# Cross-attention on one core: softmax sums inverted once for each n through DMA, and two sums of A moved to the end of batch 0's step

## The chip, the cores and the metric

The kernel runs on one core of one Trainium2 chip. The metric is the device time of an execution in microseconds (us); smaller is better. A profiled execution also has a span, from the first to the last instruction that the profiler saw on the core.

## The reference

There are eight batches. `x1` and `x2` (the context) are 512 x 1024 in float32, rows c, columns n or m. What is computed for each batch is

```
q = x1^T Wq^T + bq              # 1024 x 64
k = Wk x2 + bk                  # 64 x 1024
v = Wv x2 + bv                  # 512 x 1024
attn = softmax(q k, axis=m)     # 1024 x 1024, each row n sums to 1 over m
out = v attn^T + x1             # 512 x 1024
```

Since each row of `attn` sums to 1, the bias `bv` may be added to the output once. The kernel computes `Wv (x2 attn^T)` rather than `(Wv x2) attn^T`, with unnormalized exponentials, and multiplies by the reciprocals of the softmax sums in between. It is those reciprocals that the change is about: there is one for each n, 1024 for each batch.

## The kernel before, in words

**Two products of 2 x 2 blocks.** The product y = x2 E (E the exponentials, 1024 x 1024, indexed m by n) and the product o = Wv y are each done with seven block products instead of eight, in the Strassen-Winograd way. Block products are numbered as in the table `MULT` (L259), and done by `multiply` (L269): `first(i)` in a period is product i of y, with 4 matmuls for each of two 128 x 512 accumulators; `second(i)` is product i of o, with 2 for each. The accumulators are four PSUM banks, a0, a1, c0 and c1. Bank a is opened by products 1 of each stage and taken over by 6, 5 and 3; bank c is opened by 2, by 7, and 4 goes on in it. The sums of blocks that the products need are made on VectorE: `sum_a` (L124) makes S1, S2, S3, S4 of A (the transposed x2) for each batch, each 128 x 1024; `sum_e` (L245) makes T1 to T4 of the exponentials, `sum_y` (L251) T1 to T4 of y, and `left_sums(w, ...)` those of the weights once.

**The softmax.** n is split in halves h = 0 and 1 of 512, and m lies in partitions, eight tiles of 128. `scores` (L164) makes the scores, and ScalarE copies them to SBUF. `fold` (L194) and `fold_halves` (L203) take the maximum over tiles on VectorE, and `highest` (L207) takes it over partitions with an all-reduce on GpSimd (L210), which leaves the same 512 numbers in every partition. `exponentials` (L227) subtracts it on VectorE and takes exp on ScalarE. The sums go the same way: `sums` (L334) folds on VectorE and calls `total` (L212), which adds the halves and has GpSimd add over partitions (L215) into the tile `den`, 128 x 512, of which all partitions are alike. `shares` (L217) inverts `den` in place on VectorE with one 128 x 512 RECIPROCAL (L219); the result is called `rden`.

**Where the reciprocals are used.** `evict_y` (L294) takes a finished block of y out of PSUM in up to two steps: step 1 adds the accumulator and a temporary (L308), or for block 12 multiplies the accumulator by `rden` at once (L306); step 2 multiplies by `rden` (L310). Blocks 11 and 21 use half 0, blocks 12 and 22 half 1. `evict_o` (L319) takes blocks of o out, adding `bv` and x1 (L324) and a temporary (L331), and stores them through SP's DMA queue (L332).

**The order of the work.** The order is written out by hand, and every engine runs its own instructions in that order. `head` (L349) does batch 0's scores and half of its softmax. `period` (L431) is then called for each batch s, with n the next batch, nn and nnn those after it. In it the products of s are interleaved with the softmax of n: the scores and maxima of half 0 of n stand between first(6) and first(5) (L480 to L483), its exponentials after first(5) (L489), the scores of half 1 and the sums of half 0 of n after first(3) (L497, L498), the maxima of half 1 before first(4) (L507, L508), its exponentials among the products of o. So `total(n, 0)` of a batch is made in the period of the batch before (for batch 0 at L447), and `total(s, 1)` in its own (L463). Both halves are inverted in the period of s, after first(2): `shares(s, 0)` at L458 for batch 0 and at L461 for the others, `shares(s, 1)` at L465. In the period of batch 0 VectorE has more to do than in the others, since the rest of batch 0's softmax (`head_second`, L408) and the sums of the weights (L505) lie there. There too all four sums of A of the next batch (index 1, `sum_a` at L529) stand after second(7), and before the evictions of blocks 12 and 21 of o (L532, L534); in the later periods S1 to S3 stand after the exponentials of half 0 (L491) and S4 after the T sums of y (L503).

**Queues.** SP issues the loads of x, of A and of the old x1 (`fetch_o`) and the stores. ScalarE issues the copies of q between partitions (L156). GpSimd's own DMA queue is used twice, at the start, for the biases (L366, L367).

Of the kernel before, what the change touches and what calls it, by code (L numbers as in the profile page):

```python
# [9 lines left out]
F32 = mybir.dt.float32  # L10
# [5 lines left out]
def kernel(  # L16
# [40 lines left out]
    nc = tc.nc  # L57
    P = 128
# [3 lines left out]
    H = 512  # L62
# [3 lines left out]

    const = ctx.enter_context(tc.tile_pool(name="const", bufs=1))
    sb = ctx.enter_context(tc.tile_pool(name="sb", bufs=1))
    ps_s = ctx.enter_context(
        tc.tile_pool(name="ps_s", bufs=2, space=bass.MemoryType.PSUM)  # L70
    )
# [19 lines left out]
    def left_sums(a, *ks):  # L91

        for k in ks:
            x, y, op = {
                "S1": ("21", "22", ALU.add),
                "S2": ("S1", "11", ALU.subtract),
                "S3": ("11", "21", ALU.subtract),
                "S4": ("12", "S2", ALU.subtract),
            }[k]
            nc.vector.tensor_tensor(a["21" if k == "S3" else k], a[x], a[y], op)  # L100
            if k == "S3":
                a["S3"] = a["21"]

    class Batch:
        def __init__(self, b):
            self.b = b
            self.a, self.e, self.t, self.y, self.o = {}, {}, {}, {}, {}
            self.mx, self.top, self.den, self.rden = {}, {}, {}, {}
            self.tmp, self.bank = {}, {}

    def load_x(s, x):
# [12 lines left out]
    def sum_a(s, *ks):  # L124
        for k in ks:
            if k != "S3":
                s.a[k] = sb.tile([P, MH, C // 2], F32, tag=f"a{k}", name=f"a{k}_{s.b}")
        left_sums(s.a, *ks)
# [29 lines left out]
    def keys(s, bank=None):  # L158

        ps = project(s, "k", wk_sb, bank)  # L160
        s.k = sb.tile([P, H], F32, tag="k", name=f"k_{s.b}", bufs=2)
        nc.scalar.activation(s.k, ps, AF.Identity, bias=bk_sb)
# [31 lines left out]
    def fold(s, h, i, kind, op, ps=None):  # L194

        e = s.e[h]
        if i == 1:
            s.mx[h] = sb.tile([P, 2, H], F32, tag="fold", name=f"{kind}_{s.b}_{h}", bufs=2)
        f = s.mx[h]
        new = e[:, :, i, :] if ps is None else ps  # L200
        nc.vector.tensor_tensor(f, e[:, :, 0, :] if i == 1 else f, new, op)  # L201

    def fold_halves(s, h, op):  # L203
        f = s.mx[h]
        nc.vector.tensor_tensor(f[:, 0, :], f[:, 0, :], f[:, 1, :], op)  # L205

    def highest(s, h):  # L207
        fold_halves(s, h, ALU.max)
        s.top[h] = sb.tile([P, H], F32, tag="top", name=f"top_{s.b}_{h}", bufs=2)
        nc.gpsimd.partition_all_reduce(s.top[h], s.mx[h][:, 0, :], P, ReduceOp.max)  # L210

    def total(s, h):  # L212
        fold_halves(s, h, ALU.add)
        s.den[h] = sb.tile([P, H], F32, tag="den", name=f"den_{s.b}_{h}", bufs=3)
        nc.gpsimd.partition_all_reduce(s.den[h], s.mx[h][:, 0, :], P, ReduceOp.add)  # L215

    def shares(s, h):  # L217
        s.rden[h] = s.den[h]
        nc.vector.reciprocal(s.rden[h], s.den[h])  # L219

    def first_exponentials(s, g, i):

# [10 lines left out]
    def right_sums(t, k):  # L233

        x, y = {"T1": ("12", "11"), "T2": ("22", "T1"), "T3": ("22", "12"), "T4": ("21", "T2")}[k]
        nc.vector.tensor_tensor(t[k], t[x], t[y], ALU.subtract)  # L236

    def open_t(s):
        for n in ("T1", "T2", "T4"):
            s.t[n] = sb.tile([P, MH, H], F32, tag=f"e{n}", name=f"e{n}_{s.b}")  # L240
        e0, e1 = s.e[0], s.e[1]
        s.t |= {"11": e0[:, 0], "12": e1[:, 0], "21": e0[:, 1], "22": e1[:, 1]}
        s.t["T3"] = s.t["12"]

    def sum_e(s, *ks):  # L245
        for i in (0, 2):
            part = {n: v[:, i : i + 2, :] for n, v in s.t.items()}
            for k in ks:
                right_sums(part, k)
# [44 lines left out]
    def evict_y(s, k, steps=(1, 2)):  # L294

        bank, add = RESULT[k]
        rden = s.rden.get(int(k[1]) - 1)
        if 1 in steps:
            s.y[k] = sb.tile([P, 2, H], F32, tag=f"y{k}", name=f"y{k}_{s.b}")
        y = s.y[k]  # L300
        for step in steps:
            for j in range(2):
                ps = s.bank[bank, j]
                if add is None:
                    if step == 1:
                        nc.vector.tensor_tensor(y[:, j, :], ps, rden, ALU.mult)  # L306
                elif step == 1:
                    nc.vector.tensor_tensor(y[:, j, :], ps, s.tmp[add, j], ALU.add)  # L308
                else:
                    nc.vector.tensor_tensor(y[:, j, :], y[:, j, :], rden, ALU.mult)  # L310
# [8 lines left out]
    def evict_o(s, k):  # L319
        bank, add = RESULT[k]  # L320
        for j in range(2):
            c = 2 * (int(k[0]) - 1) + j
            o = s.o[k, j]
            nc.vector.scalar_tensor_tensor(  # L324
                o, s.bank[bank, j], bv_sb[:, c : c + 1], o, ALU.add, ALU.add
            )
        for j in range(2):
            c, h = 2 * (int(k[0]) - 1) + j, int(k[1]) - 1
            o = s.o[k, j]
            if add is not None:  # L330
                nc.vector.tensor_tensor(o, o, s.tmp[add, j], ALU.add)  # L331
            nc.sync.dma_start(out[s.b, ts(c, P), ts(h, H)], o)  # L332

    def sums(s, h):  # L334
        for i in range(1, MH):
            fold(s, h, i, "sum", ALU.add)
        total(s, h)
# [93 lines left out]
    def period(s, n, nn, nnn):  # L431

        def first(i):
            multiply(s, "y", i, s.a, s.t, MH)

        def second(i):
            multiply(s, "o", i, w, s.y, 2)

        open_t(s)
        first(1)
        if s.b == 0:
            head_second(s, n)
        sum_e(s, "T1", "T2")
        if s.b == 0:
            total(s, 0)  # L447
        else:
            sum_e(s, "T4")
        if n:  # L450
            load_a(n, "11")
        first(2)
        if s.b == 0:
            keys(n)
            load_x(nn, x1)
            evict_y(s, "11", (1,))
            sum_e(s, "T4")
            shares(s, 0)  # L458
            evict_y(s, "11", (2,))
        else:  # L460
            shares(s, 0)  # L461
            evict_y(s, "11")
        sums(s, 1)  # L463
        sum_e(s, "T3")
        shares(s, 1)  # L465
        if n:
            load_a(n, "12", "21", "22")
        first(6)

        def next_queries():  # L470
            queries(nn)
            load_x(nn, x2)

        def next_keys():
            keys(nn)
            if nnn:
                load_x(nnn, x1)

        if n:
            scores_and(n, 0, "c", next_queries if nn else nothing)  # L480
            for i in range(1, MH):
                fold(n, 0, i, "max", ALU.max)
            highest(n, 0)  # L483
        first(5)
        fetch_o(s, "11")
        fetch_o(s, "22")
        if n:
            for i in range(MH):
                exponentials(n, 0, i)  # L489
            if s.b:  # L490
                sum_a(n, "S1", "S2", "S3")  # L491
        first(7)
        evict_y(s, "22")
        first(3)
        evict_y(s, "12")
        if n:
            scores_and(n, 1, "a", next_keys if nn else nothing)  # L497
            sums(n, 0)  # L498
        sum_y(s, "T1")
        sum_y(s, "T2")  # L500
        if n:
            if s.b:
                sum_a(n, "S4")  # L503
            else:
                left_sums(w, "S1", "S2", "S3", "S4")  # L505
            for i in range(1, MH):
                fold(n, 1, i, "max", ALU.max)  # L507
            highest(n, 1)  # L508
        first(4)
        evict_y(s, "21")  # L510
        second(1)
        sum_y(s, "T3")
        sum_y(s, "T4")
        second(6)
        fetch_o(s, "12")
        if n:
            exponentials(n, 1, 0)
            exponentials(n, 1, 1)
        second(2)
        evict_o(s, "11")  # L520
        fetch_o(s, "21")
        second(5)
        if n:
            exponentials(n, 1, 2)
            exponentials(n, 1, 3)
        second(7)
        evict_o(s, "22")
        if s.b == 0:
            sum_a(n, "S1", "S2", "S3", "S4")  # L529
        if n:  # L530
            second(3)
            evict_o(s, "12")  # L532
            second(4)
            evict_o(s, "21")  # L534
        else:
            second(4)
            evict_o(s, "21")
            second(3)
            evict_o(s, "12")
# [37 lines left out]
```

## Time and profile before

| | us |
|---|---|
| median of 3 runs | 717.13 (717.1 to 717.17) |
| the profiled execution, its own time | 716.93 |
| its span | 714.9 |
| time around the span | 2.03 |
| TensorE (PE) busy in the span | 705.6 |
| VectorE (DVE) busy | 590.2 |
| ScalarE (ACT) busy | 201.3 |
| GpSimd (POOL) busy | 97.2 |

The granted TensorE clock is 1.0 throughout. Busy time is from the first to the last moment of an instruction, and matmuls overlap, so a busy TensorE need not be one at its full rate: the distance from one group's start to the next group's start tells more. "Idle before" in a row of the timeline is how long the engine stood still ahead of it, and what it was released by. The timelines of the profile are merged rows of equal instructions: start, length, engine, line, what is written from what, count.

A period of the middle batches takes 86.93 us (first(1) of one starts at 210.75, of the next at 297.68). The period of batch 0 has in addition the projections of two more batches, and lies between 26.12 and 123.72.

### The profile page before, as it was taken

What the parts mean: (1) busy time and instruction counts of PE and PEld (TensorE: products, weight loads), DVE (VectorE), ACT (ScalarE), POOL (GpSimd) and SP (SyncE); (2) the same over time, 40 slices, a digit from 0 to 9 for tenths busy, and PEclk for the clock granted to TensorE, in tenths of its full rate; (3) what the DMA queues carried; (4) which work ended last, traced back from release to release, by engine and by line L of the source; (5) the groups of instructions that cost most, each with busy time, mean ns of one, the idle gap of its engine ahead of it and who ended that gap; (6) DMA issues with size and microseconds to landing.
All of it is one profiled execution on the core that took longest, in us unless ns stands there. A gap on an engine that the chain in (4) does not pass through costs nothing.

```text
span 714.9 us, 5407 instructions
## 1 busy us (share of the span) xinstructions
PE 705.6 (99%) x1892; PEld 299.8 (42%) x1892; DVE 590.2 (83%) x569; ACT 201.3 (28%) x271; POOL 97.2 (14%) x38
## 2 busy tenths in 40 slices
PE   8999999999999999999999999999999999999997
PEld 4333444434444434444344444443434444444443
DVE  0999899988979888798887987889887898989454
ACT  2733412043211522224231232403324034220010
POOL 0132030030200211021200202002020020301000
PEclk9999999999999999999999999999999999999999
DMA  8577132441333503435133252232601350042004
GB/s 333 210 235 256 68 147 101 156 154 46 147 146 119 189 8 141 148 118 191 58 119 127 109 191 98 108 118 89 220 0 61 117 177 0 0 161 75 0 1 147
DMA packets 34699, 87.39 MB, mean 122 GB/s; under 512 B 3952, under 2 KB 3952, under 8 KB 34672
## 3 DMA queue, kind: packets, MB, share of 16 engines
q1 hardware_dynamic: 33344, 84.95, 33.6%
q10 hardware_dynamic: 1264, 2.10, 0.9%
q8 instruction: 15, 0.25, 0.1%
q14 instruction: 12, 0.10, 0.0%
q0 software_dynamic: 64, 0.00, 0.0%
HBM read 68.42 MB, written 16.78 MB: 119 GB/s over the span
## 4 chain that ended last, share of the span: by engine, by line
PE 87%; DVE 8%; DMA 1%; issue 1%; ACT 1%; SPq 0%; POOL 0%; DVEq 0%; ACTq 0%; POOLq 0%
PE ps_ya L279 27%; PE ps_yc L279 21%; PE ps_oa L279 15%; PE ps_oc L279 11%; PE ps_s L180 5%; PE ps_k L138 3%; PE ps_q L138 3%; DVE max L201 1%; DMA x_head<-in_x_dram 1%; DVE eT L236 1%; DVE e L230 1%; DVE aS L100 1%; PE ps_sa L180 1%; DVE den L219 1%; PE ps_sc L180 1%
## 5 line engine op out<-in xcount | busy, mean ns | idle before, releaser
L215 POOL PARTITION_ALL_REDUCE den<-sum x16 | 65.3, 4081 | 433.2 <-DVE sum L205 433.2
L279 PE MATMUL ps_ya<-eT,aS 128*128 128x512 f32 x256 | 113.1, 595 | 0.0
L279 PE MATMUL ps_yc<-e,a 128*128 128x512 f32 x256 | 112.6, 592 | 0.0
L289 ACT COPY uy<-ps_ya 128x512 f32<-128x512 f32 x48 | 28.1, 588 | 233.2 <-PE ps_ya L279 233.2
L230 DVE TENSOR_TENSOR e<-e,top 128x1024 f32<-128x1024 f32 x60 | 70.0, 1219 | 13.9 <-POOL top L210 13.9
L279 PEld LDWEIGHTS ps_ya<-eT,aS 128*128 128x128 f32 x256 | 48.0, 190 | 63.8 <-issue 63.6
L279 PEld LDWEIGHTS ps_yc<-e,a 128*128 128x128 f32 x256 | 48.6, 190 | 61.6 <-issue 60.1
L324 DVE SCALAR_TENSOR_TENSOR o<-ps_oc,bv_sb,o 128x512 f32<-128x512 f32 x48 | 35.7, 749 | 41.6 <-PE ps_oc L279 41.5
L231 ACT ACTIVATE e<-e 128x1024 f32<-128x1024 f32 x60 | 62.2, 1056 | 22.2 <-DVE e L230 20.4
L289 ACT COPY uo<-ps_oa 128x512 f32<-128x512 f32 x48 | 28.1, 586 | 132.4 <-PE ps_oa L279 131.1
L189 ACT COPY e<-ps_s 128x1024 f32<-128x1024 f32 x47 | 46.7, 1027 | 61.5 <-PE ps_s L180 61.5
L279 PE MATMUL ps_ya<-e,a 128*128 128x512 f32 x128 | 56.4, 594 | 1.3 <-ACT e L225 0.8
L279 PE MATMUL ps_oc<-y,w 128*128 128x512 f32 x128 | 57.5, 592 | 0.0
L279 PE MATMUL ps_oa<-yT,w_S 128*128 128x512 f32 x128 | 57.5, 592 | 0.0
L279 PE MATMUL ps_yc<-eT,a 128*128 128x512 f32 x128 | 57.0, 598 | 0.0
L279 PE MATMUL ps_ya<-e,aS 128*128 128x512 f32 x128 | 56.2, 592 | 0.0
L219 DVE RECIPROCAL den<-den 128x512 f32<-128x512 f32 x16 | 53.6, 3349 | 0.0
L180 PE MATMUL ps_s<-q,k 64*128 64x512 f32 x188 | 47.9, 608 | 1.6 <-ACT q L347 0.8
L210 POOL PARTITION_ALL_REDUCE top<-max x16 | 30.3, 1897 | 131.3 <-DVE max L205 131.3
L308 DVE TENSOR_TENSOR y<-ps_yc,uy 128x512 f32<-128x512 f32 x48 | 31.2, 676 | 15.0 <-PE ps_yc L279 14.9
L201 DVE TENSOR_TENSOR max<-max,e 128x1024 f32<-128x1024 f32 x32 | 39.2, 1225 | 3.7 <-ACT e L187 0.5
L201 DVE TENSOR_TENSOR sum<-sum,e 128x1024 f32<-128x1024 f32 x32 | 39.2, 1225 | 2.1
(65 smaller groups left out, 757.5 us busy)
## 6 DMA issues: line engine op xcount, KB each, us to landing
x_in_x_dram<-in_x_dram SPq DMA_DIRECT2D x56, 512.0 KB, 5.4
a<-in_x2T_dram SPq DMA_DIRECT2D x32, 512.0 KB, 4.2
o<-in_x_dram SPq DMA_DIRECT2D x64, 256.0 KB, 6.4
out_dram<-o SPq DMA_DIRECT2D x64, 256.0 KB, 2.1
x_head<-in_x_dram SPq DMA_DIRECT2D x8, 512.0 KB, 8.0
q<-q ACTq DMA_DIRECT2D x14, 128.0 KB, 6.9
w<-in_wvT_dram SPq DMA_DIRECT2D x4, 256.0 KB, 8.9
wqk_sb<-in_wqk_dram ACTq DMA_DIRECT2D x1, 256.0 KB, 4.7
```

The lines of the kernel that those rows point to most:

```text
L138: nc.tensor.matmul(ps[r, :], w_sb[:, c, :], s.x[:, c, ts(h, H)], start=(c == 0), stop=(c == CT - 1),)
L180: nc.tensor.matmul(ps[g], s.k[r, ts(i, P)], s.q[r, ts(h, H)], start=True, stop=True)
L189: nc.scalar.copy(e[:, :, i, :], whole)
L201: nc.vector.tensor_tensor(f, e[:, :, 0, :] if i == 1 else f, new, op)
L215: nc.gpsimd.partition_all_reduce(s.den[h], s.mx[h][:, 0, :], P, ReduceOp.add)
L219: nc.vector.reciprocal(s.rden[h], s.den[h])
L230: nc.vector.tensor_tensor(e, e, top, ALU.subtract)
L231: nc.scalar.activation(e, e, AF.Exp)
L279: nc.tensor.matmul(ps, left[ka][:, k, ts(j, P)], right[kb][:, k, :], start=opens and k == 0, stop=i in (2, 3, 4) and k == n_k - 1, skip_gr ...
L289: nc.scalar.copy(s.tmp[i, j], ps)
L308: nc.vector.tensor_tensor(y[:, j, :], ps, s.tmp[add, j], ALU.add)
L324: nc.vector.scalar_tensor_tensor(o, s.bank[bank, j], bv_sb[:, c : c + 1], o, ALU.add, ALU.add)
```

## The change

For each half of n there is now a tile `few`, 128 x 4, and a scratch row `row` of 512 numbers in DRAM (pools with two buffers each). `total` has GpSimd's DMA queue spread partition 0 of `den` over 128 partitions into `few`. `shares` inverts `few` (a 128 x 4 RECIPROCAL), writes it to `row`, and reads `row` back to all 128 partitions over `den`; both DMAs are on GpSimd's queue. The calls move. In batch 0's period step 1 of block 11's eviction stands before the keys and T4, `shares(s, 0)` comes after `sums(s, 1)`; in the others `shares(n, 0)` is called a period earlier, after the maxima of half 1, and this also holds for batch 1, in batch 0's period. `shares(s, 1)` and step 2 of block 11's eviction move behind the maxima of the next batch's half 0, ahead of first(5). S3 and S4 of the next batch's A in batch 0's period move behind the last eviction of o.

```diff
@@ class Batch
-            self.mx, self.top, self.den, self.rden = {}, {}, {}, {}
+            self.mx, self.top, self.den, self.few, self.rden = {}, {}, {}, {}, {}
...
@@ total, shares
         nc.gpsimd.partition_all_reduce(s.den[h], s.mx[h][:, 0, :], P, ReduceOp.add)
+        s.few[h] = sb.tile([P, H // P], F32, tag="few", name=f"few_{s.b}_{h}", bufs=2)
+        nc.gpsimd.dma_start(
+            s.few[h], s.den[h][0:1, :].rearrange("o (p f) -> o p f", p=P)
+        )

     def shares(s, h):
+
+        nc.vector.reciprocal(s.few[h], s.few[h])
+        row = dram.tile([1, H], F32, tag="row", name=f"row_{s.b}_{h}")
+        nc.gpsimd.dma_start(row.rearrange("o (p f) -> (o p) f", p=P), s.few[h])
         s.rden[h] = s.den[h]
-        nc.vector.reciprocal(s.rden[h], s.den[h])
+        nc.gpsimd.dma_start(s.rden[h], row.broadcast_to([P, H]))
...
@@ period
         first(2)
+        evict_y(s, "11", (1,))
         if s.b == 0:
             keys(n)
             load_x(nn, x1)
-            evict_y(s, "11", (1,))
             sum_e(s, "T4")
+        sums(s, 1)
+        if s.b == 0:
             shares(s, 0)
-            evict_y(s, "11", (2,))
-        else:
-            shares(s, 0)
-            evict_y(s, "11")
-        sums(s, 1)
         sum_e(s, "T3")
-        shares(s, 1)
...
             highest(n, 0)
+        shares(s, 1)
+        evict_y(s, "11", (2,))
         first(5)
...
             highest(n, 1)
+            shares(n, 0)
         first(4)
...
         if s.b == 0:
-            sum_a(n, "S1", "S2", "S3", "S4")
+            sum_a(n, "S1", "S2")
         if n:
             second(3)
             evict_o(s, "12")
             second(4)
             evict_o(s, "21")
+            if s.b == 0:
+                sum_a(n, "S3", "S4")
         else:
```

More of the change, by code (lines that the diff above doesn't have):

```diff
@@ L68 @@
     sb = ctx.enter_context(tc.tile_pool(name="sb", bufs=1))
+    dram = ctx.enter_context(
+        tc.tile_pool(name="dram", bufs=2, space=bass.MemoryType.DRAM)
+    )
     ps_s = ctx.enter_context(
@@ L215, in total @@
         nc.gpsimd.partition_all_reduce(s.den[h], s.mx[h][:, 0, :], P, ReduceOp.add)
+        s.few[h] = sb.tile([P, H // P], F32, tag="few", name=f"few_{s.b}_{h}", bufs=2)
+        nc.gpsimd.dma_start(
+            s.few[h], s.den[h][0:1, :].rearrange("o (p f) -> o p f", p=P)
+        )
     def shares(s, h):
+        nc.vector.reciprocal(s.few[h], s.few[h])
+        row = dram.tile([1, H], F32, tag="row", name=f"row_{s.b}_{h}")
+        nc.gpsimd.dma_start(row.rearrange("o (p f) -> (o p) f", p=P), s.few[h])
         s.rden[h] = s.den[h]
-        nc.vector.reciprocal(s.rden[h], s.den[h])
+        nc.gpsimd.dma_start(s.rden[h], row.broadcast_to([P, H]))
     def first_exponentials(s, g, i):
```

## The prediction

> **What bounds the kernel now.** I read the page's busy shares first, then the chain that ended last, then TensorE's timeline at the places where that chain leaves TensorE, set against the same places of a middle batch.
>
> ```profile
> span 714.9 us, 5407 instructions
> ...
> PE 705.6 (99%) x1892; PEld 299.8 (42%) x1892; DVE 590.2 (83%) x569; ACT 201.3 (28%) x271; POOL 97.2 (14%) x38
> ...
> L219 DVE RECIPROCAL den<-den 128x512 f32<-128x512 f32 x16 | 53.6, 3349 | 0.0
> ```
>
> TensorE is busy all the time, so the 53.6 us of reciprocals on VectorE cannot simply come off. The question is where TensorE still loses time. The chain of waits, in order of time:
>
> ```profile
> 78.41 1.00 issue
> 79.41 3.49 DVE e L230 x3
> 82.89 1.20 DVE y L308 x2
> 84.09 1.20 DVE y L310 x2
> 85.29 0.61 DVE y L306
> 85.95 1.29 PE ps_sa L180 x3
> ...
> 123.00 0.67 DVE o L324
> 123.72 7.13 PE ps_ya L279 x16
> ```
>
> Until 85.95 the chain runs mostly over VectorE; then over TensorE, broken once at 123. From 123.72 on it is TensorE alone until 710.54, with one group behind the next. So the middle batches hold nothing to gain, and I look at batch 0. TensorE's timeline, batch 0 first and then a middle batch:
>
> ```profile
> 83.76 1.99 PE L180 MATMUL ps_s<-q,k 64*128 64x512 f32 x8
> 85.95 1.29 PE L180 MATMUL ps_sa<-q,k 64*128 64x512 f32 x3 [0.20 <-DVE y L306]
> ...
> 92.04 7.13 PE L279 MATMUL ps_yc<-eT,a 128*128 128x512 f32 x16
> ```
>
> ```profile
> 346.39 1.99 PE L180 MATMUL ps_s<-q,k 64*128 64x512 f32 x8
> 348.21 1.02 PE L180 MATMUL ps_sa<-q,k 64*128 64x512 f32 x4
> ...
> 353.61 7.13 PE L279 MATMUL ps_yc<-eT,a 128*128 128x512 f32 x16
> ```
>
> The same scores and keys take 92.04 - 83.76 = 8.28 us in batch 0 and 353.61 - 346.39 = 7.22 in the other. The rows name only 0.20 of wait; the distance between starts says 1.06, lost because both banks a are emptied late by block 12's eviction (L306). In the same way second(3), second(4) and first(1) of batch 1 run from 116.18 to 130.69, 14.51 us, against 377.75 to 391.49, 13.74: 0.77 lost, where first(1) waits for L324, block 12's output, which stands on VectorE behind four sums of A (118.25 to 123.0). The rest of batch 0's groups have the middle batch's lengths but for 0.2 us at the keys at 44.89. **So 1.06 + 0.77 = 1.83 us can be had**, and nothing at the start (to 26.12) or at the end is touched.
>
> **What the Trainium skill says.** "DMA: Bandwidth & Descriptors", section "Anatomy of one DMA": a DMA from GpSimd's queue costs about 2.0 us fixed, mostly the receipt of its last write. The trace agrees only for an idle DMA; from issue to landing it has
>
> ```profile
> out_dram<-o SPq DMA_DIRECT2D x64, 256.0 KB, 2.1
> ...
> bqk_sb<-in_bqk_dram POOLq DMA_DIRECT2D x1, 1.0 KB, 6.0
> ```
>
> The second row moves a kilobyte while the engines of the DMA were full (share 1.03 at 5 to 10 us). Same page, "Two DMAs through the same engine are not ordered": a DMA that reads what another wrote must wait for its semaphore, so few, row and the broadcast are hops in series, and the broadcast holds GpSimd's queue until the row has landed. No run shows this yet. "SBUF — State Buffer", section "Who interferes with whom": a VectorE instruction with two SBUF inputs contends with a GpSimd one that reads SBUF. The trace agrees: an eT sum takes 1.22 us alone and 3.15 (at 92.18) beside an all-reduce of 4.14 us.
>
> **The change, part by part.** Times below are of the profiled execution.
>
> *Removed:* 16 RECIPROCALs, 2 x 3.35 us in each batch on VectorE. *Added there:* 2 of 128 x 4. The trace has none; the slope is 3349/512 = 6.5 ns a column, so four columns cost 0.03 us over the instruction's own cost, at most the 0.17 of the memset. I take 0.1. VectorE gains 6.5 us a batch, worth nothing to TensorE in middle batches.
>
> *Added on GpSimd:* three DMA issues per half, 48 in all. The two issues of before took 0.86 and 0.55 us; I take 0.86, 41 us in total, beside 617 us of idle time. Issues of the broadcast have 128 rows of 2 KB and could take longer; the landing below is bounded from 2.1 to 6.0 per hop and counts from the issue. The broadcasts add 16 x 256 KB = 4.2 MB to 87.4 MB. No matmul waited for a DMA after 12.49, so I cost the traffic at nothing; if a load came late it would cost its lateness.
>
> *New waits, middle batch* (times of the batch at 297.68). (a) `few` of half 0 of the next batch: its all-reduce ends at 355.94, at 6.0 it lands at 361.9. The RECIPROCAL stands ahead of block 21's eviction, at 361.68 now: 0.3 us late. Behind it are block 21's two steps (2.4 us), and second(2), which needs that block and its bank, starts at 367.45: slack is 367.45 - 364.08 = 3.4 us. The DMA share is 0.93 at 355 to 360, so I take 6.0. Cost nothing; TensorE's earlier products hide it, up to a landing at 365.1, 9.1 us after the all-reduce. (b) `few` of half 1: the all-reduce comes 1.2 us earlier, ends at 321.0 and lands by 327.0 at worst; VectorE, done with the maxima by 325.6, would wait at most 1.4 us where today it stands 1.99 for `top`. The row is issued behind that all-reduce (ends at about 327.5), under load lands at 333.5, the broadcast at 339.5; block 22's second step wants it at 340.1. In time even at 6.0 a hop. (c) The broadcast of half 0 has a whole period.
>
> *Batch 0, first place.* VectorE without the two reciprocals and with step 2 of block 11 later: T4 ends at 55.15, the folds of half 1 take 4.4, to 59.5. `few` 0, all-reduced by 54.0, lands between 56.1 and 60.0 (DMA share 0.96, 0.89): RECIPROCAL done by 60.1. T3 (4.3 with its contention), then maxima (4.5), to about 69. GpSimd: all-reduce of half 1 59.7 to 63.8, `few` 1 issued to 64.7, row 0 issued there, landing 66.8 to 70.7; only then the broadcast, landing 68.9 to 76.7. Block 11's step 2 stands on VectorE right ahead of the exponentials of the next batch and waits for it; `highest`, behind the broadcast's issue on GpSimd, is through by 73.4. Step 2 takes 1.2, so the exponentials start between 70.8 (an early `highest` then decides) and 77.9, against 78.26 now. From there to the end of L306's first instruction it is 85.90 - 78.26 = 7.64. Even at the slow end bank a0 is free at 77.9 + 7.64 = 85.54, and the scores want it at 83.76 + 1.82 = 85.58. DMA share is 0.99 and 0.95 from 65 to 75 and 0.00 after, so I take a value between, a broadcast at 74: exponentials at 75.2, block 12 waiting for its product and not for VectorE. **Gain 1.06.** For the row and broadcast of half 1, from 73.4, the DMA is idle: 79.4 + 2.1 = 81.5 at most, wanted at 80.9 to 83.6 by block 22's step 2. Here the margin is thin, but 2.1 for both gives 77.6.
>
> *Batch 0, second place.* Without S3 and S4 (1.15 + 1.22 us) L324 of block 12 starts at 120.65 rather than 122.92, its second ends at 122.0, and bank a is wanted at 119.61 + 3.43 = 123.04. **Gain 0.77.** VectorE's earlier savings do not help or harm here, because it waits for TensorE at 114.67 and 116.38 anyway. S3 and S4 then follow block 21's output, at about 125.2; T1 and T2 of batch 1 start at 127.6 rather than 126.75. They are wanted by first(6) at 137.5, and T3, T4 and S later. What is late next: nothing, as 3.35 us of reciprocal has gone from the stretch before first(6). SP's stores of block 12 are issued 2.3 us earlier, nothing is put ahead of a load.
>
> *Last batch.* The sum's all-reduce ends at about 661.6, three hops at 2.1 and issues give 670, at 6.0 each 681; wanted at 673.45. Block 22's step 1 frees its bank before that wait, and second(1) uses only block 11. At the slow end T1 and T2 of y come late for second(6) at 689.7 by nothing (681 + 1.2 + 1.3 + 2.4 = 686). Cost nothing.
>
> The sum: 716.93 - 1.06 - 0.77 = 715.10 on the profiled execution, which lies 0.2 under the median of the runs. Against the median, 717.13 - 1.83 = **715.3**, 0.26% faster.
>
> **The rivals.** *Only the moved sums count* (0.17): hops at 6.0 and a bit over, block 11's step 2 holds the exponentials to 78.3 or so, and the 1.06 stays. Then 717.13 - 0.77 = 716.4. For it: the DMA is full to 75; against it: the broadcast must land after 76.7, and by the Trainium skill (same page, "Queues, rings and completion order") each DMA engine takes turns between its queues, which lets a small transfer in; no run shows that yet. *A new wait takes the place* (0.13): broadcast at 77.8 or later, exponentials 0.8 us later than now; 716.4 + 0.8 = 717.2. The same holds if the head's own scatter hides the gain. *Slower* (0.08): `few` of half 0 lands after the 9.1 us of (a). At a landing after 10.6 us every one of the seven periods with a next batch loses 1.5 us: 717.13 - 1.83 + 7 x 1.5 = 725.8. It decides from 9.1 us on; for it speaks that VectorE's sums and SP's loads are on at that time, against it that the slowest small DMA of before took 6.0. That the change does not do what it says is no case: the built order has the reciprocals at 128 x 4 and the calls where the diff puts them.
>
> **How the numbers follow.** The full gain has 0.62, the others 0.17, 0.13 and 0.08. The full gain and the moved sums leave 0.21 out, so the range reaches into the third case: 714.8 (half a microsecond of scatter under the forecast) to 717.2. This kernel's measurement tells about 0.2% from no change, 1.43 us, so faster means under 715.70, near the forecast: of the first case I give 0.60 to it. Slower needs over 718.56: the last case and the far end of the third, 0.09. The rest, 0.31, is the same.
>
> **What would show it.** In the profile after: scores to products at the first place 7.2 us apart, not 8.3; no wait of first(1) for L324 in batch 1; no reciprocal over 0.2 us; middle periods still 86.93; the landing of the new DMAs between 2.1 and 6.0; the exponentials of the next batch in batch 0 before 77.9. Wrong would be a wait of VectorE for a DMA of GpSimd's queue that ends in a wait of TensorE, or periods longer than 86.93.

## The result, and the profile after

| | before | after |
|---|---|---|
| median of 18 runs each | 717.17 (717.07 to 718.74) | 715.92 (714.91 to 717.94) |
| ratio | | 0.9982, 95% interval 0.9976 to 0.9988 |
| the profiled execution, its own time | 716.93 | 715.50 |
| its span | 714.9 | 713.7 |
| time around the span | 2.03 | 1.80 |

The change is 1.25 us faster, 0.18%, where 1.83 us, 0.26%, were forecast. The 715.92 lies inside the forecast range of 714.8 to 717.2, 0.62 above the full gain's 715.3 and 0.48 under the 716.4 of the first rival, and above the 715.70 under which most of the chance had been put. A few runs of the kernel before, and of some of the others, lie some 1.5 us above the rest of their kernel; they are left in the medians. Apart from these the runs of before lie within 0.33 us (717.07 to 717.40), while those after spread over 2.0 (714.91 to 716.91).

Line numbers below are those of the kernel named. In the changed kernel L226 is the small RECIPROCAL, L220 the DMA to `few`, L228 that to `row`, L230 the broadcast, L241 the exponentials' subtraction, L321 step 2 of an eviction, L317 block 12's eviction, L213 the maximum's all-reduce, L335 the output's eviction. The page of after:

```profile
span 713.7 us, 5497 instructions
...
PE 704.5 (99%) x1892; PEld 299.5 (42%) x1892; DVE 546.6 (77%) x569; ACT 200.1 (28%) x271; POOL 124.1 (17%) x86
...
L321 DVE TENSOR_TENSOR y<-y,den 128x512 f32<-128x512 f32 x48 | 35.7, 786 | 4.8 <-DMA den<-row 4.8
```

VectorE lost 43.6 us of work: its reciprocals fell from 53.6 to 2.8 us, but the multiplications by the reciprocals rose from 30.8 to 35.7. TensorE's busy time fell by 1.1. The third row has a wait that is new: step 2 once waited 4.8 us for a broadcast. The chain that ended last, over the two places of the prediction:

```profile
77.13 6.87 PE ps_ya L290 x16
84.00 1.92 PE ps_s L183 x8
85.91 0.85 PE ps_sa L183 x2
...
122.77 6.87 PE ps_ya L290 x16
```

It is TensorE throughout; the VectorE pieces of before are gone. TensorE's timeline there:

```profile
83.92 1.99 PE L183 MATMUL ps_s<-q,k 64*128 64x512 f32 x8
85.75 1.06 PE L183 MATMUL ps_sa<-q,k 64*128 64x512 f32 x3
...
91.61 7.13 PE L290 MATMUL ps_yc<-eT,a 128*128 128x512 f32 x16
...
115.74 3.60 PE L290 MATMUL ps_oa<-y,w_S 128*128 128x512 f32 x8
...
122.61 7.03 PE L290 MATMUL ps_ya<-e,a 128*128 128x512 f32 x16
```

The second place in the kernel before, for comparison:

```profile
116.18 3.60 PE L279 MATMUL ps_oa<-y,w_S 128*128 128x512 f32 x8
...
123.72 7.13 PE L279 MATMUL ps_ya<-e,a 128*128 128x512 f32 x16 [0.51 <-DVE o L324]
```

**First place** (scores and keys): 91.61 - 83.92 = 7.69, was 8.28, undisturbed 7.22. It gained 0.59 of the 1.06. **Second place**: first(1) of batch 1 starts 6.87 after second(3), was 7.54; with the 0.10 that the group after a stall takes longer, all of the 0.77. The rest of the 1.43 between the two profiled executions: 0.23 less around the span, and 0.16 lost in the head (26.21 for 26.12) and at the keys at 45 (3.86 for 3.79). From first(1) of batch 1 to the start of the last product both kernels take the same but for that 0.10: 583.09 us after, 583.19 before.

Why the first place is not whole is seen on VectorE,

```profile
59.61 0.17 DVE L226 RECIPROCAL few<-few 128x4 f32<-128x4 f32 x1
...
67.90 0.69 DVE L208 TENSOR_TENSOR max<-max 128x512 f32<-128x512 f32 x1
71.66 0.18 DVE L226 RECIPROCAL few<-few 128x4 f32<-128x4 f32 x1 [3.06 <-DMA few<-den]
76.62 1.29 DVE L321 TENSOR_TENSOR y<-y,den 128x512 f32<-128x512 f32 x2 [4.79 <-DMA den<-row]
77.83 4.63 DVE L241 TENSOR_TENSOR e<-e,top 128x1024 f32<-128x1024 f32 x4
...
84.77 1.28 DVE L317 TENSOR_TENSOR y<-ps_ya,den 128x512 f32<-128x512 f32 x2
```

and on GpSimd:

```profile
64.28 0.55 POOL L220 DMA_DIRECT2D few<-den  x1 [0.30 <-POOL den L218]
64.83 0.55 POOL L228 DMA_DIRECT2D row<-few  x1
72.92 0.54 POOL L230 DMA_DIRECT2D den<-row  x1 [7.55 <-DMA row<-few]
73.49 1.74 POOL L213 PARTITION_ALL_REDUCE top<-max  x1
```

VectorE stands still for 3.06 + 4.79 = 7.85 us. It is through with the maxima at 68.6; the row, issued at 64.83, lets the broadcast go only at 72.92, and that lands at 76.6. The exponentials start at 77.83, just 0.43 before those of the kernel before:

```profile
64.11 4.40 DVE L236 TENSOR_TENSOR e<-e 128x1024 f32<-128x1024 f32 x2
68.45 3.35 DVE L219 RECIPROCAL den<-den 128x512 f32<-128x512 f32 x1
...
78.26 4.63 DVE L230 TENSOR_TENSOR e<-e,top 128x1024 f32<-128x1024 f32 x4 [2.00 <-POOL top L210]
```

### The profile page after: what moved, and what is told of

It reads as the page before. It is cut to its first block, busy times and chain, and to the rows that moved or that the text cites. A ratio compares the mean times of both kernels' runs of the same rounds, so it can differ in the third digit from the quotient of the medians.

```text
span 713.7 us, 5497 instructions
## 1 busy us (share of the span) xinstructions
PE 704.5 (99%) x1892; PEld 299.5 (42%) x1892; DVE 546.6 (77%) x569; ACT 200.1 (28%) x271; POOL 124.1 (17%) x86
## 4 chain that ended last, share of the span: by engine, by line
PE 95%; DMA 2%; DVE 1%; SPq 1%; ACT 0%; issue 0%; DVEq 0%; ACTq 0%
PE ps_ya L290 31%; PE ps_yc L290 22%; PE ps_oa L290 15%; PE ps_oc L290 12%; PE ps_s L183 6%; PE ps_q L141 4%; PE ps_k L141 3%; DMA x_head<-in_x_dram 1%; DMA x_in_x_dram<-in_x_dram 1%; PE ps_sa L183 1%; PE ps_sc L183 1%; DVE aS L103 0%; DVE max L204 0%; SPq L388 0%; SPq L118 0%
## 5 line engine op out<-in xcount | busy, mean ns | idle before, releaser
L241 DVE TENSOR_TENSOR e<-e,top 128x1024 f32<-128x1024 f32 x60 | 70.0, 1219 | 1.4 <-POOL top L213 1.4
L335 DVE SCALAR_TENSOR_TENSOR o<-ps_oc,bv_sb,o 128x512 f32<-128x512 f32 x48 | 35.8, 750 | 38.9 <-PE ps_oc L290 38.9
L213 POOL PARTITION_ALL_REDUCE top<-max x16 | 32.8, 2047 | 95.6 <-DVE few L226 47.9
L321 DVE TENSOR_TENSOR y<-y,den 128x512 f32<-128x512 f32 x48 | 35.7, 786 | 4.8 <-DMA den<-row 4.8
```

Of the source, the lines that this page charges most:

```text
L241: nc.vector.tensor_tensor(e, e, top, ALU.subtract)
L335: nc.vector.scalar_tensor_tensor(o, s.bank[bank, j], bv_sb[:, c : c + 1], o, ALU.add, ALU.add)
```

## The experiments

The detour is what the three DMAs of a half do: to `few`, to `row` and back to `den`; each of them is a hop. The theory: *the gain is one of order, at two places of batch 0; what is missing of it, and the spread of the runs, come from the hops that hold the exponentials there*. The rivals: the moved sums alone gain; VectorE's saved time gains; the detours of all batches cost and scatter. Ratios are against runs of the kernel before on the same chip.

**The moved sums alone**, on the kernel before:

```diff
-            sum_a(n, "S1", "S2", "S3", "S4")
+            sum_a(n, "S1", "S2")
...
             evict_o(s, "21")
+            if s.b == 0:
+                sum_a(n, "S3", "S4")
```

> The kernel before, with only S3 and S4 of batch 1 moved behind the last eviction of o. Hop theory (the detour's missing gain lies in batch 0's wait for the broadcast of half 0, and the moved sums give their full 0.77 us): 717.2 - 0.77 = 716.4, ratio 0.9989, the runs within 0.3 us of each other as before the change, first(1) of batch 1 no longer waiting for the output of block 12. Rival, the moved sums are the whole of the change's gain: 715.9, ratio 0.9982. Rival, the loss returns at the first sums of batch 1: ratio 1.000.

Measured: 716.64, ratio 0.9990 (0.9982 to 0.9998). TensorE's timeline:

```profile
83.69 1.99 PE L180 MATMUL ps_s<-q,k 64*128 64x512 f32 x8
86.07 1.29 PE L180 MATMUL ps_sa<-q,k 64*128 64x512 f32 x3 [0.39 <-DVE y L306]
...
92.17 7.13 PE L279 MATMUL ps_yc<-eT,a 128*128 128x512 f32 x16
...
116.30 3.60 PE L279 MATMUL ps_oa<-y,w_S 128*128 128x512 f32 x8
...
123.17 7.03 PE L279 MATMUL ps_ya<-e,a 128*128 128x512 f32 x16
```

The second place is whole (6.87), the first still loses (8.48). The sums are not the whole gain. The expectation on the spread was wrong: 10 of 13 runs lie within 0.65 us, and three are 1.0 to 1.5 us above the median.

**The detour without the moved sums**: the changed kernel with `sum_a(n, "S1", "S2", "S3", "S4")` back in its place.

> The changed kernel with S3 and S4 back ahead of the evictions of blocks 12 and 21. Hop theory: 715.9 + 0.77 = 716.7, ratio 0.9993, and the runs scatter by 2 to 3 us, since the scatter comes from the hops. Moved sums as the whole gain: 717.2, ratio 1.000. If the scatter of the changed kernel is gone here, it came from the moved sums and the hop theory falls.

Measured: 716.63, ratio 0.9995 (0.9987 to 1.0003). The first place takes 7.83, the second 7.54 as before. Near the 716.7 expected; the interval includes no change, so by itself this does not part the theories. The runs lie over 2.65 us, but three of the 13 are 1.5 us and more above the median, like some of the kernel before; the other ten lie within 1.12. So the spread doesn't part them either.

**Step 2 behind the exponentials** in batch 0, on the changed kernel:

```diff
         shares(s, 1)
-        evict_y(s, "11", (2,))
+        if s.b:
+            evict_y(s, "11", (2,))
...
                 exponentials(n, 0, i)
+            if s.b == 0:
+                evict_y(s, "11", (2,))
```

> The changed kernel, but in batch 0 step 2 of block 11's eviction stands behind the four exponentials of the next batch and not ahead of them. Hop theory: the broadcast no longer holds them, but the maximum's all-reduce still stands behind the broadcast's issue on GpSimd, so they start near 75.3; bank a is free in time, 715.3 to 715.5, ratio 0.9974 to 0.9977, with less scatter than the changed kernel but not none, as a row that lands 2 us later still holds the all-reduce. Traffic rival: as the changed kernel, 715.9 with its scatter.

Measured: 715.19 (714.86 to 715.49, 6 runs), ratio 0.9967 (0.9955 to 0.9979). VectorE:

```profile
75.86 4.63 DVE L241 TENSOR_TENSOR e<-e,top 128x1024 f32<-128x1024 f32 x4 [5.67 <-POOL top L213]
80.41 1.28 DVE L321 TENSOR_TENSOR y<-y,den 128x512 f32<-128x512 f32 x2
```

The exponentials now wait for the maximum, which stood behind the broadcast's issue on GpSimd (issued at 73.52, all-reduce from 74.09), but no longer for its landing. TensorE:

```profile
84.41 1.99 PE L183 MATMUL ps_s<-q,k 64*128 64x512 f32 x8
...
91.63 7.13 PE L290 MATMUL ps_yc<-eT,a 128*128 128x512 f32 x16
```

The first place takes 7.22. All 16 detours are still there, the missing gain has come, and the six runs lie within 0.63 us.

**Half 0 of batch 0 in full on VectorE**, on the changed kernel, twice:

```diff
     def shares(s, h):
+        if (s.b, h) == (0, 0):
+            s.rden[h] = s.den[h]
+            nc.vector.reciprocal(s.rden[h], s.den[h])
+            return
```

(and `total` leaves out the DMA to `few` there)

> The changed kernel, but half 0 of batch 0 alone is inverted on VectorE in full (128 x 512, in place, 3.35 us), with no hop; the other 15 go by DMA. Hop theory: VectorE waited 7.9 us for those hops, so 3.35 us more of work costs nothing; the exponentials of batch 1 start near 73.5 and not at 77.8, the whole 1.06 us at the scores comes, 715.3, ratio 0.9974, and the runs lie within 0.5 us. Rival, traffic (the DMAs of all batches and GpSimd's issues cost and scatter): 715.9 to 716.0 with 2 to 3 us of scatter, as the changed kernel. Rival, half 1's hops take over the wait: the eviction of block 22 waits for its broadcast, 715.6 or more, with the scatter.

Measured: 715.90, ratio 0.9982 (0.9973 to 0.9990), but in two groups of six runs, 714.75 to 715.33 and 716.47 to 717.05. The profiled execution is one of the lower group: exponentials at 72.04, first place 7.22. To see whether the upper group is half 1's hops or the chip's, again:

> Once more the changed kernel with half 0 of batch 0 alone inverted in full, whose runs fell into two groups, near 715.1 and near 716.8. If the upper group comes from half 1's hops, both groups come again, and a profile that falls into the upper one shows VectorE held ahead of block 22's second step beyond 80.1 and the first place longer than 7.22. If the groups are the chip's: one group, near 715.1.

Measured: 715.18 (714.83 to 715.24, 6 runs), ratio 0.9969 (0.9957 to 0.9981), first place 7.22. One group, on another chip. So 3.35 us more of VectorE's work costs nothing there and gains the rest of the first place; where the upper group of the first twelve runs came from stays open, since no execution of it was profiled. It is also the one case without the wait for half 0's broadcast in which the runs spread over 2 us.

**Both halves of batch 0 in full**, 14 detours left (`if s.b == 0:` in the place of the condition above):

> The changed kernel, with both halves of batch 0 inverted in full on VectorE, and by DMA in the other seven batches. Hop theory, now with half 1's hops as a second wait: 715.2, ratio 0.997, and no run above 716 but for those 1.5 us up that the kernel before has too. Rival, the detour of the other batches costs or scatters: 715.9 or runs spread over 2 us, since 14 of the 16 detours are left. The two theories part on the spread more than on the median.

Measured: 715.22 (715.00 to 715.48, 6 runs), ratio 0.9970 (0.9959 to 0.9982), first place 7.22. As the theory had it: the detours of the other batches neither cost nor scatter.

**The order alone**, all reciprocals in full, no DMA. Against the changed kernel, with the lines of the three DMAs, which go too, left out:

```diff
     def shares(s, h):
-        nc.vector.reciprocal(s.few[h], s.few[h])
...
         s.rden[h] = s.den[h]
+        nc.vector.reciprocal(s.rden[h], s.den[h])
...
         sums(s, 1)
-        if s.b == 0:
-            shares(s, 0)
+        shares(s, 0)
...
             highest(n, 1)
-            shares(n, 0)
```

> The new order of the calls with all reciprocals in full on VectorE and no DMA: half 0 after the folds of half 1, half 1 ahead of step 2 of block 11, in every batch, and the moved sums. VectorE has its 53.6 us of reciprocals again. Hop theory: the gain is one of order; in batch 0 the exponentials start near 76 (step 2 and half 1's reciprocal fill the time in which VectorE waited for the maximum), both places gain in full, 715.3, ratio 0.9974, and the runs lie within 0.3 us of each other. Rival, VectorE's saved time is what gains: 716.4, ratio 0.9989 (moved sums alone), or slower if the exponentials come late in the middle batches.

Measured: 715.22 (714.88 to 715.47, 5 runs), ratio 0.9968 (0.9955 to 0.9980). VectorE:

```profile
63.09 2.29 DVE L236 TENSOR_TENSOR e<-e 128x1024 f32<-128x1024 f32 x2
...
69.82 3.34 DVE L219 RECIPROCAL den<-den 128x512 f32<-128x512 f32 x1
73.08 1.22 DVE L310 TENSOR_TENSOR y<-y,den 128x512 f32<-128x512 f32 x2
74.22 4.62 DVE L230 TENSOR_TENSOR e<-e,top 128x1024 f32<-128x1024 f32 x4
...
81.16 0.68 DVE L306 TENSOR_TENSOR y<-ps_ya,den 128x512 f32<-128x512 f32 x1
84.21 0.69 DVE L306 TENSOR_TENSOR y<-ps_ya,den 128x512 f32<-128x512 f32 x1 [2.37 <-PE ps_ya L279]
```

The second reciprocal and step 2 fill the time in which the maximum is made on GpSimd. The exponentials start at 74.22, 3.6 us sooner than in the changed kernel, though VectorE does 53.5 us of reciprocals again. Block 12 waits for TensorE, not TensorE for it: the first place takes 7.22, the second 6.87.

The order does one thing more, which the expectation did not have. The reciprocal of half 0 (59.83 to 63.17) now runs beside the all-reduce of half 1 (60.01 to 63.24), and the sum T3 behind them takes 2.29 us. In the kernel before and in the changed one T3 runs beside that all-reduce and takes 4.40 and 4.37. So 3.34 us of reciprocal there delay the maxima by only 1.1. Counted from the end of T4, the exponentials come 4.4 us sooner than in the kernel before (74.22 - 55.45 against 78.26 - 55.14): about 2 us are T3's, and about 2 the filled wait for the maximum.

**Batch 0's order alone**, on the kernel before, sums of A where they were:

```diff
-            shares(s, 0)
-            evict_y(s, "11", (2,))
...
         sums(s, 1)
+        if s.b == 0:
+            shares(s, 0)
         sum_e(s, "T3")
-        shares(s, 1)
+        if s.b:
+            shares(s, 1)
...
             highest(n, 0)
+        if s.b == 0:
+            shares(s, 1)
+            evict_y(s, "11", (2,))
```

> The kernel before with only the order in batch 0 changed (half 0's reciprocal after the folds of half 1, half 1's and step 2 of block 11 after the maxima of the next batch), reciprocals in full, sums of A where they were, all other batches as before. Hop theory, the first place's 1.06 us is one of order: 717.2 - 1.06 = 716.15, ratio 0.9985, with the wait of first(1) for L324 left. Rival, VectorE's shorter reciprocals are needed for it: 717.2, ratio 1.000.

Measured: 716.20 (21 runs), ratio 0.9985 (0.9978 to 0.9991).

```profile
84.12 1.99 PE L180 MATMUL ps_s<-q,k 64*128 64x512 f32 x8
...
91.34 7.13 PE L279 MATMUL ps_yc<-eT,a 128*128 128x512 f32 x16
...
123.01 7.13 PE L279 MATMUL ps_ya<-e,a 128*128 128x512 f32 x16 [0.50 <-DVE o L324]
```

The first place is whole, 7.22, with reciprocals as long as before; the second's wait is left. Moving three calls in one batch gives the 1.06.

**Two more hops** for half 0 of batch 0, on the changed kernel:

```diff
+        if (s.b, h) == (0, 0):
+            for k in range(1):
+                x = dram.tile([1, H], F32, tag="more", name=f"more_{k}")
+                nc.gpsimd.dma_start(x.rearrange("o (p f) -> (o p) f", p=P), s.few[h])
+                nc.gpsimd.dma_start(s.few[h], x.rearrange("o (p f) -> (o p) f", p=P))
         row = dram.tile([1, H], F32, tag="row", name=f"row_{s.b}_{h}")
```

> The changed kernel, with two more hops for half 0 of batch 0 alone (to a second scratch row and back to the 128 x 4 tile, ahead of the row). Hop theory: the broadcast lands 4 to 5 us later, the exponentials of batch 1 with it, and TensorE loses it one for one at the scores and what follows: 715.9 + 4.5 = 720.4, ratio 1.0045. Rival, the wait is hidden by TensorE's queue of work: 715.9, ratio 0.998.

Measured: 723.25 (4 runs), ratio 1.0077 (1.0061 to 1.0092), where 720.4 was expected. VectorE, then TensorE:

```profile
82.68 1.29 DVE L326 TENSOR_TENSOR y<-y,den 128x512 f32<-128x512 f32 x2 [12.35 <-DMA den<-row]
83.90 4.62 DVE L246 TENSOR_TENSOR e<-e,top 128x1024 f32<-128x1024 f32 x4
```

```profile
84.28 1.99 PE L183 MATMUL ps_s<-q,k 64*128 64x512 f32 x8
91.57 2.67 PE L183 MATMUL ps_sa<-q,k 64*128 64x512 f32 x4 [5.30 <-DVE y L322]
```

The broadcast landed 6.1 us later (expected 4 to 5), and the time grew by 7.3: lateness there is not hidden at all, and here it cost more than itself. The first place takes 15.48. Behind its stop of 5.30 us, two groups of four score matmuls take 2.67 and 2.51 us, where the undisturbed ones take 1.02, and the granted clock, 1.00 from 84 to 88, is 0.71, 0.50 and 0.94 in the next three stretches of 4 us, then 1.00 again. So TensorE went on slower for some microseconds after the long stop; in the changed kernel, with its short stop, the clock is 1.00 from 80 to 90.

**Less load on the DMA** in batch 0's stretch, on the changed kernel:

```diff
         first(5)
-        fetch_o(s, "11")
-        fetch_o(s, "22")
+        if s.b:
+            fetch_o(s, "11")
+            fetch_o(s, "22")
...
             scores_and(n, 1, "a", next_keys if nn else nothing)
+            if s.b == 0:
+                fetch_o(s, "11")
+                fetch_o(s, "22")
```

> The changed kernel, but in batch 0 the loads of old x1 for blocks 11 and 22 (1 MB) are issued behind batch 3's first load of x, some 25 us later, so the DMA's full stretch at 63 to 76 is shorter by about 3 us. If it is the load that stretches the hops of half 0: row lands near 69.9 rather than 72.9, the broadcast near 73, exponentials near 74.3, full gain, 715.3, ratio 0.9974, less scatter. Rival, the hops are slow in themselves beside VectorE's work (descriptors): row still takes 8 us, 715.9 with the scatter. If an output waits for the later load: slower, with a wait of L335 for a DMA.

Measured: 714.70 (714.62 to 715.43, 5 runs), ratio 0.9963 (0.9951 to 0.9976). The time came, the mechanism did not: in the profiled execution (715.01) the DMA's full stretch ended at 72 instead of 76, but that still covers the hop of the row (share 1.02 from 65 to 70), so the broadcast was issued at 72.80 (72.92 in the changed kernel) and the first place took 7.60. The load was taken off too late in the stretch to test what stretches the row. Whether the other runs had earlier landings was not seen.

The changed kernel's own trace tells more. Two hops of a row in a middle batch, each from its issue to the issue of the broadcast that waits for it:

```profile
327.12 0.56 POOL L228 DMA_DIRECT2D row<-few  x1
333.80 0.54 POOL L230 DMA_DIRECT2D den<-row  x1 [6.11 <-DMA row<-few]
...
362.22 0.56 POOL L228 DMA_DIRECT2D row<-few  x1
364.48 0.54 POOL L230 DMA_DIRECT2D den<-row  x1 [1.69 <-DMA row<-few]
```

The first took 6.68 us with a DMA share of 0.98, the second 2.26 with 0.01; VectorE was busy nearly all the time in both (6.23 of 6.5 us, 2.50 of 2.5). All 16 rows divide in this way: six lie in stretches with a share of 0.98 or more and take 6.7 to 8.1, ten in stretches with a share of at most 0.29 and take 2.0 to 3.0. So it is the load that goes with a slow hop, and not VectorE's work.

The same later loads without a detour, and with step 2 behind the exponentials:

> The new order with full reciprocals and no DMA detour, and batch 0's loads of old x1 for blocks 11 and 22 issued later, as in the run with less load. If the later loads helped only through the hops of the detour: 715.2, as the order alone. If they help in themselves (another transfer that TensorE or VectorE waits for): 714.7.

Measured: 715.37 (715.17 to 715.82, 7 runs), ratio 0.9971 (0.9961 to 0.9982). Later loads gain nothing by themselves.

> The changed kernel with both edits that took the wait for the broadcast off: in batch 0 step 2 of block 11 behind the exponentials, and the loads of old x1 for blocks 11 and 22 issued later. Hop theory: each of the two already gave the whole gain at the scores, so together they give no more, 715.2, ratio 0.9971 with less than 1 us between the runs. If the 714.7 of the run with less load was more than chance, and comes from the load beside the detour: 714.7.

Measured: 714.70 (714.57 to 714.95, 6 runs), ratio 0.9966 (0.9954 to 0.9978). The theory's 715.2 missed by 0.5, as in the run with less load. Both profiled executions have a first place or head no better than others; they are 0.3 us shorter after the last product's start (7.67 and 7.72, against 7.94 to 8.00 in all others). Why the later loads together with the detour shorten the last store is not known. Of all the versions these two have the lowest medians; the order alone, with 715.22, comes within about 0.5 us of them without any scratch row.

## Why the prediction was nearly right

*Where the gain can be: right.* The two places of batch 0 are all that changed inside the span, up to the scatter of the head; middle batches kept 86.93 us (first(1) at 296.47 and at 383.40).

*The second place, 0.77: right to the hundredth*, in the changed kernel and with the moved sums alone (6.87 for 7.54, and 0.10 in the group after).

*The first place, 1.06: mechanism right, two terms mis-sized.* The first is the time of the hops. I bounded a hop by 6.0 us and took a broadcast landing at 74. The row took 8.1 from its issue to the broadcast's, and `few` of half 1, issued at 64.28, 7.4 to VectorE's use of it. The landing at 76.6 kept inside my bound of 76.7 only because the broadcast itself took 3.7 rather than 6.0. The DMA share over these times:

```profile
65.00:70.00 5.00, 5.00 (x13) 2.23 (x12) 3.35 (x4) 0.59 (x1) 0.37 (x1) 1.00 1.03 306
70.00:75.00 5.00, 5.00 (x13) 2.27 (x12) 0.18 (x1) 0.59 (x1) 2.05 (x2) 1.00 1.04 350
```

(The last two columns are the DMA's share and GB/s.) The Trainium skill's fixed 2.0 us for a DMA ("DMA: Bandwidth & Descriptors", "Anatomy of one DMA") holds here as the price in an idle stretch, where the row issued at 103.70 let its broadcast go 2.2 us later, at a DMA share of 0.02; at full load the row took four times that. (The 2.1 from which the prediction took its lower bound was that of SP's stores, not of GpSimd's queue.) That a small transfer is let in between the loads, which was held against the first rival, showed only in part: the row was through by 72.92, some 3 us before the loads ended near 76, but 8.1 us after its issue.

The second term is the point from which lateness costs. I held that exponentials at 77.9 cost nothing, because bank a0 would be free at 85.54. They started at 77.83 and 0.47 was lost. I had looked at the first of block 12's two instructions. Weight loads of the changed kernel:

```profile
85.51 0.42 PEld L183 LDWEIGHTS ps_sa<-q,k 64*128 64x128 f32 x2 [0.43 <-DVE y L317]
86.11 0.18 PEld L183 LDWEIGHTS ps_sa<-q,k 64*128 64x128 f32 x1 [0.17 <-DVE y L317]
```

The second bank comes with the second instruction, which ended at 86.05. And a stop there costs more than the wait that is named for it: before, 0.20 was named and 1.06 lost. The measure is the lead, the time from the start of the exponentials on VectorE to that of the scores on TensorE: 5.30 us cost 1.26 (moved sums alone: 78.39 to 83.69), 5.50 cost 1.06 (before), 5.93 cost 0.61 (detour alone), 6.09 cost 0.47 (after), 6.17 cost 0.38 (less load), 9.88 nothing (order alone). My figures put the point at a lead of 83.76 - 77.9 = 5.86. By estimate, following these costs to zero, it lies near 6.5; two thirds of a microsecond of the margin was not there.

*The sum* had 1.83; the profiled execution gave 0.59 + 0.77 + 0.23 - 0.16 = 1.43, and the median 0.18 less than that. The 0.23 around the span was not foreseen; it made up for half of the missing 0.47, and that much of the forecast's nearness is luck. The median lies 0.7 above the 715.2 of four variants without the wait, and the runs spread over 2 us. Lateness of the hops that passes on undamped would do both, but it was not seen in an unprofiled run, so the cause of the spread is argued and not shown.

*Middle batches: right.* `few` of half 0 held VectorE for 0.68 us in the batch of the prediction, where 0.3 was forecast, and for at most 1.08 in the other middle batches, inside 3.4 of slack:

```profile
361.15 0.18 DVE L226 RECIPROCAL few<-few 128x4 f32<-128x4 f32 x1 [0.68 <-DMA few<-den]
```

The row of half 1 took 6.7 (issued 327.12, broadcast issued 333.80) where 6.0 was the bound, and up to 7.9 in other batches (414.06 to 421.99). It still came in time: no step 2 outside batch 0 waited for a broadcast.

*The signs.* Of those that the prediction had set, these came: no wait of first(1) for block 12's output, no reciprocal over 0.2 us, middle periods of 86.93, and, by 0.07, exponentials before 77.9. These did not: 7.2 at the first place (7.69), and landings of at most 6.0. And what it had named as the sign of being wrong was there, in small: VectorE waited 4.79 for the broadcast, the exponentials and block 12's eviction came late by it, and TensorE's loads for the scores waited for that eviction.

*The rivals.* That the moved sums alone count did not hold, since the first place gained 0.59; but the way in which that rival had the 1.06 stay, step 2 holding the exponentials, is what kept 0.47 of it. The slower case did not occur: the slowest hop to `few` was used 7.7 after its all-reduce, under the 9.1. The sum of 3.15 us at 92.18, which the prediction calls one of E, is one of y (yT in the trace); the reading of its length stands.

*What the forecast did not see*: the detour was not needed. It let the first place's gain come from the two reciprocals gone from VectorE and from step 2 moved, together, and never asked what the order gives with the reciprocals left in. It gives at least as much: the exponentials start 3.6 us sooner, and the first place is whole.

## What to carry to other kernels

A short DMA chain cost about 2 us a hop here and up to 8 where bulk loads were in flight; put what waits for it behind the work that others need, or do the work in place when the engine would stand idle anyway. Before taking an instruction off a busy engine, try moving it into that engine's own waits, or to where it keeps two engines from slowing each other: here the order alone came to 0.9968 (0.9955 to 0.9980), the change to 0.9982 (0.9976 to 0.9988); the two intervals overlap by a little. And take the margin at the last of the instructions that free a buffer, not at the first.

## What the runs showed that was not expected

- Time around the span is 2.01 to 2.06 us in the five profiled executions without the detour (before, moved sums, order alone, order with less load, batch 0's order), and 1.73 to 1.83 in the nine with it. The cause was not looked for.
- A 128 x 4 RECIPROCAL takes 0.17 us, of which the next instruction waits only 0.09 (59.61 to 59.70).
- GpSimd's issue of any of the new DMAs, 16 bytes or 2 KB a row, takes 0.54 to 0.56 us.
- The keys of batch 1 at 45 took 3.58 to 4.15 us in the fourteen profiled executions, with a wait for the load of x named in two (batch 0's order alone, and the later loads with the later step 2); with the head (26.00 to 26.45) this is most of the scatter that is left.
